# Expanding the last 64 channels for two phases in one step, and issuing every rearrangement copy from SyncE

## The chip, the cores and the metric

The kernel runs on one core of one Trainium2 chip. The metric is the device time of one launch in microseconds (us). The kernel before the change takes 4784.22 us, the median of three runs (4777.77 to 4787.7). A core has five engines with an instruction stream of their own: TensorE (PE in the profile; PEld are its weight loads), VectorE (DVE), ScalarE (ACT), GpSimd (POOL) and SyncE (SP), which issues transfers and computes nothing. Each engine works through its instructions in order and waits where an instruction needs something that isn't there yet.

## The reference

Two residual blocks are applied to 32 images of 96 channels, 56 x 56, in fp32. The first is an inverted bottleneck with weights and activations quantised to 4 bits; the second mixes channels in three ways (a gated 3x3 convolution, a fractional Fourier transform, a Fourier transform) and ends in a dense 3x3 convolution.

```python
# block 1, on _gn(x) (normalised in groups of three channels)
h = bn(conv(x, quant_w(w1), b1, 1, 0, 1), g1, be1, m1, v1)      # 1x1, 96 -> 576
h = act_q(h)                                                    # clip to 0..1, 15 levels
h = bn(conv(h, quant_w(w2), b2, 1, 1, HID), g2, be2, m2, v2)    # 3x3 depthwise, 576
h = act_q(h)
h = bn(conv(h, quant_w(w3), b3, 1, 0, 1), g3, be3, m3, v3)      # 1x1, 576 -> 96
x = x + (_gn(x) + h)
# block 2, on _gn(x), channels in three thirds
#   x_0: 3x3 convolution with gated weights
#   x_05: fractional Fourier transform, 1x1 mix, inverse transform, magnitude
#   x_1: rfft2, 1x1 mix, irfft2
out = conv3x3(concat([x_0, IFRFT, x_1])) + conv2_b
x = x + out
```

## The kernel before

An image is cut into four phases (even and odd rows and columns), 28 x 28 = 784 points each. The 576 hidden channels are cut into five blocks: four of 128 and a last one of 64 (`blk(b)` gives the size). `expand(b, k)` makes block b of phase k. The input is split into a high and a low part, `vh` and `vl`, and both are multiplied by `w1`, so there are 2 x 2 matmuls with 392 columns each. ScalarE evicts the result with scale, offset and Relu (tile `qt`, shown as `qte`), VectorE clips it at 15 and writes it as fp8 into one of three buffers `q1s`. Transfers then rearrange it: the depthwise convolution wants 32 channels of all four phases on 128 partitions, so each group of 32 channels goes into the partitions of its phase in `qp`. Groups are issued from SyncE and GpSimd in turn. For the last block the weight matrix is filled up with zeros to 128 columns, so its steps make 64 channels and 64 rows of nothing.

```python
# weights, once
w1 = cp.tile([C, NB * 128], F32R, tag="w1r", name="w1r")
nc.vector.memset(w1f[:, HID:], 0.0)
nc.vector.tensor_copy(w1, w1f)

def expand(b, k):
    ps = pair(f"pe{i}_{b}_{k}")                       # 2 banks of PSUM; 2 such pairs in all
    for n, v in enumerate((s["vh"], s["vl"])):
        for h in range(2):
            nc.tensor.matmul(ps[:, h, :HN], w1[:, 128 * b : 128 * (b + 1)],
                v[:, k, HN * h : HN * (h + 1)], start=(n == 0), stop=(n == 1))
    src = q1s[turn["q1s"] % 3]
    turn["q1s"] += 1
    quant_act(ps, A1[:, b : b + 1], B1[:, b : b + 1], src[:, :, :PH], f"e{i}_{b}_{k}")
    n, at = blk(b) // G, PW * (k // 2) + k % 2
    for g in range(n):
        (nc.gpsimd if g % 2 else nc.sync).dma_start(
            out=qps[(NB * i + b) % 3][G * k : G * (k + 1), g, at : at + PH * PW],
            in_=src[g * G : (g + 1) * G].rearrange("c h w -> c (h w)"))
```

`depthwise(b, j)` (tile `pd`) reads `qp`, `project` (tile `pp`) comes last in the block. The second block of one image is interleaved with the first block of the next. Its pieces that matter here are these:

```python
def group_stats(stats, name):        # means and 1/std of a group of channels
    ...
    nc.vector.tensor_scalar(ve, pv[:C, 0:1], 1e-5, None, ALU.add)
    nc.gpsimd.tensor_tensor(rstd, ve, mhalf, ALU.pow)      # GpSimd
    ...
def angles():                        # ends with four small transfers
    ...
    nc.sync.dma_start(out=s["xf"][at : at + 1]..., in_=vv[...])
def mix_f(j):                        # matmul pm<-xf,g; two buffers zs; DRAM tile z
    ...
        nc.sync.dma_start(out=s["z"][:, h, at], in_=t)     # z<-zs, 8 per image
    ...
        nc.sync.dma_start(out=zh[...], in_=z[...]...)      # zh<-z, 2 per image
        nc.sync.dma_start(out=az[...], in_=src[r])         # az<-z, 8 per image
# rows_f: matmul pi<-cs,zh, copies to Y;  columns_f: matmul pz<-cs,Y, squares sq, sums Z
# magnitude: four ACT square roots cat<-Z;  final(j): 9 matmuls pc<-cat,wc, x 7 per image
```

The order of the steps:

```python
ex = [(0.75, lambda b=b, k=k: expand(b, k)) for b in range(NB) for k in range(4)]   # 20
de = [(1.45, lambda g=g: depthwise(g // 4, g % 4)) for g in range(NG0)]             # 18
for g in range(NG0):
    conv += de[g : g + 1] + ex[LEAD + g : LEAD + g + 1]                             # LEAD = 7
...
at = 2 * (4 * NB - LEAD) + 1
conv[at:at] = nxt["split"]           # vh and vl of the next image, behind the last expand
```

The framework that builds the program may still move instructions when it lays them out, with a timing model of its own.

Of the kernel before, what the change touches and what calls it, by code (L numbers as in the profile page):

```python
# [37 lines left out]
F32 = mybir.dt.float32  # L38
F32R = mybir.dt.float32r
# [8 lines left out]
C, H, W = 96, 56, 56  # L48
HW = H * W
HID = 576  # L50
NB = 5
# [3 lines left out]
G = 32  # L55
NG0 = HID // G
PH = H // 2
PN = PH * PH
PW = PH + 2
PT = (PH + 1) * PW + 2  # L60
HN = PN // 2
HH = HW // 2
LOW = 64
LEAD = 7
# [13 lines left out]
def blk(b):  # L78
    return 128 if b < NB - 1 else HID - 128 * (NB - 1)


def view(ap, offset, dims):

    return bass.AP(ap.tensor, ap.offset + offset, [list(ap.ap[0])] + [list(d) for d in dims])
# [19 lines left out]
def block_kernel(ctx: ExitStack, tc: tile.TileContext, out: bass.AP, a: dict):  # L104
    nc = tc.nc
# [3 lines left out]
    cp = ctx.enter_context(tc.tile_pool(name="const", bufs=1))  # L109
# [11 lines left out]
    def pair(name):  # L121

        return ps0.tile([128, 2, 512], F32, tag="pair", name=name)
# [4 lines left out]
    def load(i):  # L128
        xt = xp.tile([C, HW], F32, tag="x", name=f"x{i}")
        nc.sync.dma_start(out=xt, in_=x_in[i].rearrange("c h w -> c (h w)"))  # L130
        xts[i] = xt
# [4 lines left out]
    def const(name, eng=nc.scalar):  # L136
        src = a[name]
        t = cp.tile(list(src.shape), F32, tag=name, name=name)
        eng.dma_start(out=t, in_=src)
        return t  # L140

    gmat = const("gmat")
    def prepare():

        room = p1.tile([128, NG0 * PN // 2], F32, tag="q2", name="prep")
        used = [0]

        def tmp(p, n):
            used[0] += n
            return room[:p, used[0] - n : used[0]]  # L150

        def load_tmp(name):
            src = a[name]
            t = tmp(*src.shape)
            nc.scalar.dma_start(out=t, in_=src)
            return t

        def quantise(w, p, n, name):

            w = w[:, :n]  # L160
            nc.scalar.activation(w, w, AF.Tanh)
            mx = tmp(p, 1)
            nc.vector.tensor_reduce(mx, w, AX.X, ALU.max, apply_absolute_value=True)
            am = tmp(p, 1)
            nc.gpsimd.partition_all_reduce(am, mx, p, bass_isa.ReduceOp.max)
            rc = tmp(p, 1)
            nc.vector.tensor_scalar(am, am, 2.0, None, ALU.mult)
            nc.vector.reciprocal(rc, am)
            nc.vector.tensor_scalar(w, w, rc, 0.5, ALU.mult, ALU.add)
            nc.vector.tensor_scalar(w, w, 15.0, MAGIC, ALU.mult, ALU.add)  # L170
            nc.vector.tensor_scalar(w, w, MAGIC, 2.0, ALU.subtract, ALU.mult)
            nc.vector.tensor_scalar(w, w, 15.0, None, ALU.subtract)

        w1f = load_tmp("w1")
        quantise(w1f, C, HID, "1")
        w1 = cp.tile([C, NB * 128], F32R, tag="w1r", name="w1r")
        nc.vector.memset(w1f[:, HID:], 0.0)
        nc.vector.tensor_copy(w1, w1f)
        w2 = load_tmp("w2")
        quantise(w2, 128, NG0 * 16, "2")  # L180
        mask = load_tmp("mask")
        w2v = view(w2, 0, [[16, NG0], [1, 16]])
        nc.vector.tensor_tensor(w2v, w2v, view(mask, 0, [[0, NG0], [1, 16]]), ALU.mult)
        w3f = load_tmp("w3")
        quantise(w3f, 128, NG0 * C, "3")
        w3 = cp.tile([128, NG0, C], BF16, tag="w3q", name="w3q")
        nc.vector.tensor_copy(w3, w3f.rearrange("p (g c) -> p g c", c=C))


        ident4 = load_tmp("ident4")  # L190
        dw = cp.tile([128, NG0, 4, 128], FP8, tag="dw", name="dw")
        for g in range(NG0):
            nc.vector.tensor_tensor(
                view(dw[:, g].rearrange("p t o -> p (t o)"), 0, [[G, 16], [1, G]]),
                view(ident4, 0, [[0, 16], [1, G]]),
                view(w2, 16 * g, [[1, 16], [0, G]]),
                ALU.mult,
                saturate=False,
            )


        v1 = load_tmp("vec1")
        v2 = load_tmp("vec2")
        v3 = load_tmp("vec96")

        def batchnorm(v, p, n, name):
            col = lambda k: v[:, k * n : (k + 1) * n]
            s = cp.tile([p, n], F32, tag=f"s{name}", name=f"s{name}")
            o = cp.tile([p, n], F32, tag=f"o{name}", name=f"o{name}")
            nc.vector.tensor_scalar(s, col(4), BN_EPS, None, ALU.add)  # L210
            nc.scalar.activation(s, s, AF.Sqrt)
            nc.vector.reciprocal(s, s)
            nc.vector.tensor_tensor(s, s, col(1), ALU.mult)
            nc.vector.tensor_tensor(o, col(0), col(3), ALU.subtract)
            nc.vector.tensor_tensor(o, o, s, ALU.mult)
            nc.vector.tensor_tensor(o, o, col(2), ALU.add)
            return s, o

        A1, B1 = batchnorm(v1, 128, NB, "1")
        nc.vector.tensor_scalar(B1, B1, 15.0, None, ALU.mult)  # L220
        A2, B2 = batchnorm(v2, 128, NG0, "2")
        nc.vector.tensor_scalar(A2, A2, 1.0 / 15.0, None, ALU.mult)
        nc.vector.tensor_scalar(B2, B2, 15.0, None, ALU.mult)
        A3, B3 = batchnorm(v3, C, 1, "3")
        nc.vector.tensor_scalar(A3, A3, 1.0 / 225.0, None, ALU.mult)


        def signed(name, factor):
            w = const(name)
            f = load_tmp(factor)  # L230
            nc.vector.tensor_tensor(w, w, f, ALU.mult)
            return w

        cw = signed("cw", "coef")
        return w1, dw, w3, A1, B1, A2, B2, A3, B3, cw

    w1, dw, w3, A1, B1, A2, B2, A3, B3, cw = prepare()
# [14 lines left out]
    q1s, qps = [], []  # L252
# [57 lines left out]
    def quant_act(ps, scale, offset, dst, name):  # L310

        t = p3.tile([128, PN], I16, tag="qt", name=f"qt{name}")
        nc.scalar.activation(t.rearrange("p (h n) -> p h n", h=2), ps[:, :, :HN], AF.Relu, bias=offset, scale=scale)  # L313
        src = t if len(dst.shape) == 2 else t.rearrange("p (h w) -> p h w", w=PH)
        nc.vector.tensor_scalar(dst, src, 15.0, None, ALU.min, saturate=False if dst.dtype == FP8 else None)  # L315
# [9 lines left out]
    def layer0(i):  # L325

        xt = xts[i]
        s = {}
# [37 lines left out]
            nc.vector.tensor_scalar(xt, xt, s["one"], s["off"], ALU.mult, ALU.add)  # L366

        def expand(b, k):
            ps = pair(f"pe{i}_{b}_{k}")
            for n, v in enumerate((s["vh"], s["vl"])):  # L370
                for h in range(2):
                    nc.tensor.matmul(  # L372
                        ps[:, h, :HN],
                        w1[:, 128 * b : 128 * (b + 1)],
                        v[:, k, HN * h : HN * (h + 1)],
                        start=(n == 0),
                        stop=(n == 1),
                    )
            src = q1s[turn["q1s"] % 3]
            turn["q1s"] += 1  # L380
            quant_act(ps, A1[:, b : b + 1], B1[:, b : b + 1], src[:, :, :PH], f"e{i}_{b}_{k}")

            n, at = blk(b) // G, PW * (k // 2) + k % 2
            for g in range(n):
                (nc.gpsimd if g % 2 else nc.sync).dma_start(  # L385
                    out=qps[(NB * i + b) % 3][G * k : G * (k + 1), g, at : at + PH * PW],
                    in_=src[g * G : (g + 1) * G].rearrange("c h w -> c (h w)"),
                )

        def depthwise(b, j):  # L390
            g = 4 * b + j
# [38 lines left out]
                nc.vector.bn_stats(stats2[i][:, j, :], xt[:, j * CN : (j + 1) * CN])  # L430


        ex = [(0.75, lambda b=b, k=k: expand(b, k)) for b in range(NB) for k in range(4)]
        de = [(1.45, lambda g=g: depthwise(g // 4, g % 4)) for g in range(NG0)]
        conv = []
        for g in range(NG0):
# [339 lines left out]
    for i in range(B):  # L776
        conv, nxt = now["conv"], None
        if i + 1 < B:
            nxt = layer0(i + 1)
            conv[8:8] = nxt["norm"]  # L780
            at = 2 * (4 * NB - LEAD) + 1
            conv[at:at] = nxt["split"]


        interleave(conv, one[:-4])
        interleave(now["last"], one[-4:-2])
        head, two, done = layer1(i)
        interleave(head + (nxt["first"] if nxt else []), one[-2:] + end)
        if i + 2 < B:
            load(i + 2)  # L790
        one, end, now = two, done, nxt
# [86 lines left out]
def _layout(inputs):  # L878
# [3 lines left out]
    f = np.float32  # L882
    k = _constants()
# [2 lines left out]

    def hidden(v):

        p = np.zeros((NB * 128,) + v.shape[1:], f)
        p[:HID] = v  # L890
        return np.moveaxis(p.reshape((NB, 128) + v.shape[1:]), 0, 1)

    k["x"] = np.asarray(inputs["x"])
# [34 lines left out]
    start = {"alpha": G, "gfreq": G, "gsp": 0, "gfft": 2 * G}  # L928
# [5 lines left out]
    at = [("gfreq", 0, 64, GO_F), ("gsp", 0, 32, GO_S), ("gfft", 0, 64, GO_T)]  # L934
    at += [("gfreq", 64, 128, GI_F), ("gsp", 32, 64, GI_S), ("gfft", 64, 128, GI_T)]
    for name, lo, hi, to in at:
        n = mlps.index(name)
# [35 lines left out]
```

## Time and profile before

| | value |
|---|---|
| time, median of 3 | 4784.22 us (4777.77 to 4787.7) |
| span of the profiled run, mean granted TensorE clock | 4769.9 us, 0.942 |
| ACT evictions qte of the expand steps | 640, 999 ns mean |
| DVE conversions q1s of the expand steps | 640, 559 ns mean |
| copies qp<-q1s, from SyncE and from GpSimd | 1152 and 1152, 26.2 KB each |
| TensorE matmuls of the expand steps | 2560 (1280 with vh, 1280 with vl) |

The page of the profile gives busy time for each engine and then the groups of instructions: source line, engine, operation, and the tiles in the form written<-read. The waits give, for an instruction, the instruction whose end released it, with the total, the number and the longest. "issue" means that nothing in the profile held the engine back. The granted clock is the share of full speed at which TensorE's clock ran. SPq and POOLq are the queues in which SyncE and GpSimd issue transfers.

### The profile page before, as it was taken

How to read it: one execution, taken by the hardware profiler on the slowest of the kernel's cores; microseconds unless marked ns; L12 is line 12 of the kernel's file. 1: busy time of each engine (PE TensorE's matmuls, PEld its weight loads, DVE VectorE, ACT ScalarE, POOL GpSimd, SP SyncE). 2: the span in 40 equal slices, each digit the busy share in tenths (PEclk: the TensorE clock that was granted, in tenths of full speed). 3: DMA queues.
4: the chain of work that ended last, by engine and by line, in shares of the span. 5: the costliest groups of instructions: out<-in, count | busy, mean ns of one | idle time of the engine just before them, and what ended most of it. 6: DMA issues, size and time to landing. Idle time of an engine off the chain costs nothing.

```text
span 4769.9 us, 60944 instructions
## 1 busy us (share of the span) xinstructions
PE 4327.5 (91%) x21632; PEld 2494.2 (52%) x21632; DVE 2387.7 (50%) x5385; ACT 2166.3 (45%) x2824; POOL 861.2 (18%) x1361
## 2 busy tenths in 40 slices
PE   3899999899999999998999999999999999989987
PEld 2555555555555555555555555455555455555544
DVE  5545544545455555545445454555455444554532
ACT  3544445544445444445444454444454444553431
POOL 3221111221102211112211022111122111122110
PEclk9999999999999999989999989999999999999998
DMA  2221122221122211222211223112222112222112
GB/s 72 44 64 45 38 52 61 65 63 39 35 57 65 64 51 35 48 61 64 63 32 41 58 64 64 43 42 49 61 64 64 45 28 58 63 64 56 30 34 48
DMA packets 378818, 249.65 MB, mean 52 GB/s; under 512 B 283233, under 2 KB 371668, under 8 KB 372372
## 3 DMA queue, kind: packets, MB, share of 16 engines
q1 hardware_dynamic: 339072, 211.72, 20.1%
q0 software_dynamic: 36864, 31.04, 2.8%
q8 instruction: 174, 2.85, 0.3%
q10 hardware_dynamic: 2580, 2.99, 0.2%
q14 instruction: 128, 1.05, 0.1%
HBM read 92.90 MB, written 89.92 MB: 38 GB/s over the span
## 4 chain that ended last, share of the span: by engine, by line
PE 59%; DMA 11%; ACT 10%; DVE 10%; issue 7%; SPq 1%; POOL 1%; DVEq 0%; ACTq 0%; POOLq 0%
PE pc L746 29%; PE pd L398 12%; PE pp L414 5%; PE pe L372 4%; DMA zh<-z 4%; DMA z<-zs 3%; PE pi L678 3%; ACT cat L720 2%; DMA xf<-vv 2%; PE pm L653 2%; ACT qte L313 2%; ACT qtd L313 2%; DVE q1s L315 1%; PE px L616 1%; ACT xm L471 1%
## 5 line engine op out<-in xcount | busy, mean ns | idle before, releaser
L746 PE MATMUL pc<-cat,wc 96*96 96x448 f32 x4032 | 1644.1, 564 | 55.9 <-ACT cat L720 55.9
L385 POOL DMA_DIRECT2D qp<-q1s x1152 | 620.7, 543 | 3621.2 <-issue 1631.1
L746 PEld LDWEIGHTS pc<-cat,wc 96*96 96x96 f32 x4032 | 672.2, 170 | 906.5 <-issue 824.5
L313 ACT ACTIVATE qtd<-pd,o,s 128x784 int16<-128x784 f32 x576 | 576.4, 1001 | 949.8 <-PE pd L398 903.4
L398 PE MATMUL pd<-qp,dw 128*128 128x392 fp8e4 x4608 | 948.6, 350 | 43.3 <-ACT qtd L313 42.0
L313 ACT ACTIVATE qte<-pe,o,s 128x784 int16<-128x784 f32 x640 | 639.2, 999 | 625.5 <-PE pe L372 608.9
L398 PEld LDWEIGHTS <-dw 128*128 128x128 fp8e4 x4608 | 448.0, 101 | 510.5 <-issue 267.9
L372 PE MATMUL pe<-vh,w1r 96*128 96x392 f32 x1280 | 432.1, 420 | 117.4 <-ACT qte L313 63.5
L315 DVE TENSOR_SCALAR q1s<-qte 128x784 fp8e4<-128x784 int16 x640 | 357.4, 559 | 170.8 <-ACT qte L313 120.6
L754 DVE SCALAR_TENSOR_TENSOR x<-pc,bc,x 96x448 f32<-96x448 f32 x224 | 152.3, 680 | 574.5 <-PE pc L746 571.8
L315 DVE TENSOR_SCALAR q<-qtd 128x784 bf16<-128x784 int16 x576 | 207.4, 360 | 406.0 <-ACT qtd L313 405.9
L372 PE MATMUL pe<-vl,w1r 96*128 96x392 f32 x1280 | 352.7, 358 | 0.0
L372 PEld LDWEIGHTS pe<-vh,w1r 96*128 96x128 f32 x1280 | 226.1, 199 | 239.2 <-issue 101.6
L414 PE MATMUL pp<-q,w3q 32*96 32x392 bf16 x4608 | 256.1, 328 | 2.2 <-DVE x L426 2.2
L653 PE MATMUL pm<-xf,g 34*128 34x392 f32 x512 | 202.1, 617 | 56.6 <-DMA xf<-vv 52.8
L372 PEld LDWEIGHTS pe<-vl,w1r 96*128 96x128 f32 x1280 | 246.7, 199 | 0.5
L426 DVE SCALAR_TENSOR_TENSOR x<-pp,s,x 96x392 f32<-96x392 f32 x256 | 142.3, 616 | 176.0 <-PE pp L414 176.0
L414 PEld LDWEIGHTS <-w3q 32*96 32x96 bf16 x4608 | 181.1, 118 | 86.5 <-issue 32.5
L726 PE MATMUL ps<-xq,g 128*128 128x392 f32 x512 | 202.0, 537 | 0.0
L678 PE MATMUL pi<-cs,zh 120*120 120x112 f32 x1024 | 142.3, 302 | 50.3 <-DMA zh<-z 47.2
L361 ACT CAST vh<-v 96x392 fp32r<-96x392 f32 x256 | 126.2, 516 | 130.5 <-DVE v L353 129.7
L333 DVE BATCH_NORM_STATS2 bn<-x 96x6 f32<-96x448 f32 x224 | 121.1, 608 | 123.0 <-DMA x<-in_x_dram 123.0
(150 smaller groups left out, 4072.5 us busy)
## 6 DMA issues: line engine op xcount, KB each, us to landing
z<-zs SPq DMA_DIRECT2D x256, 196.0 KB
x<-in_x_dram SPq DMA_DIRECT2D x32, 1176.0 KB
out_dram<-x SPq DMA_DIRECT2D x32, 1176.0 KB
qp<-q1s SPq DMA_DIRECT2D x1152, 26.2 KB
qp<-q1s POOLq DMA_DIRECT2D x1152, 26.2 KB, 1.9
zh<-z SPq DMA_DIRECT2D x64, 392.0 KB
az<-z SPq DMA_DIRECT2D x256, 98.0 KB
xf<-vv SPq DMA_DIRECT2D x128, 6.1 KB
```

Source lines behind the costliest of these rows:

```text
L313: nc.scalar.activation(t.rearrange("p (h n) -> p h n", h=2), ps[:, :, :HN], AF.Relu, bias=offset, scale=scale)
L315: nc.vector.tensor_scalar(dst, src, 15.0, None, ALU.min, saturate=False if dst.dtype == FP8 else None)
L372: nc.tensor.matmul(ps[:, h, :HN], w1[:, 128 * b : 128 * (b + 1)], v[:, k, HN * h : HN * (h + 1)], start=(n == 0), stop=(n == 1),)
L385: (nc.gpsimd if g % 2 else nc.sync).dma_start(out=qps[(NB * i + b) % 3][G * k : G * (k + 1), g, at : at + PH * PW], in_=src[g * G : (g + 1 ...
L398: nc.tensor.matmul(ps[:, h, :HN], dw[:, g, t, :], view(qps[(NB * i + b) % 3][:, j, :], at, [[PW, PH // 2], [1, PH]]), start=(t == 0), stop ...
L414: nc.tensor.matmul(s["pp"][k // 2][:C, k % 2, :HN], w3[rows, g, :], s["q2"][rows, g, HN * h : HN * (h + 1)], start=(g == 0), stop=(g == NG ...
L426: nc.vector.scalar_tensor_tensor(part, src, A3, part, ALU.mult, ALU.add)
L653: nc.tensor.matmul(ps[:, :HN], g1[rows], s["xf"][rows, at], start=True, stop=True)
L678: nc.tensor.matmul(ps[: LOW + W, 2 * W * k : 2 * W * (k + 1)], zh[:, c : c + 2, :].rearrange("p c w -> p (c w)")[:, : LOW + W], cs, start= ...
L726: nc.tensor.matmul(ps[:, :HN], s["g0"][:, 128 * k : 128 * (k + 1)], view(xq, PH // 2 * h * (W + 2) + k, [[W + 2, PH // 2], [2, PH]]), star ...
L746: nc.tensor.matmul(ps[:C, :CN], wc[:, C * t : C * (t + 1)], cat[:, CR * j + dy : CR * j + dy + CR, dx : dx + W], start=(t == 0), stop=(t = ...
L754: nc.vector.scalar_tensor_tensor(part, ps[:C, :CN], bc, part, ALU.add, ALU.add)
```

## The change

The last block has 64 channels, so two phases of it fit into 128 rows. The new step accumulates both phases in one PSUM pair: for phase k it uses weights with the 64 channels in the left half and zeros in the right, for phase k+1 zeros on the left and the channels on the right. One buffer `w1`, with 64 zero columns on each side of the 64 channels, gives both by a shift of 64 columns. A step of the last block then has 8 matmuls, one eviction and one conversion for two phases, and four copies. The expand steps go from 20 to 18 per image. The scales and offsets of the last block are given twice. All copies are issued from SyncE, GpSimd issues none any more, and the memory kept for GpSimd's transfer descriptors is cut down. The list of steps is two shorter, so the next image's split moves up with it. The aim is fewer evictions and conversions.

```diff
-        w1 = cp.tile([C, NB * 128], F32R, tag="w1r", name="w1r")
-        nc.vector.memset(w1f[:, HID:], 0.0)
-        nc.vector.tensor_copy(w1, w1f)
+        w1 = cp.tile([C, NB * 128 + 64], F32R, tag="w1r", name="w1r")
+        nc.vector.memset(w1[:, HID - 64 :].bitcast(F32), 0.0)
+        nc.vector.tensor_copy(w1[:, : HID - 64], w1f[:, : HID - 64])
+        nc.vector.tensor_copy(w1[:, HID : HID + 64], w1f[:, HID - 64 : HID])
...
         def expand(b, k):
             ps = pair(f"pe{i}_{b}_{k}")
-            for n, v in enumerate((s["vh"], s["vl"])):
+            m = blk(b)
+            n = 128 // m
+            for e in range(2 * n):
                 for h in range(2):
+                    at = 128 * b + m * (n - 1) * (1 - e // 2)
                     nc.tensor.matmul(
                         ps[:, h, :HN],
-                        w1[:, 128 * b : 128 * (b + 1)],
-                        v[:, k, HN * h : HN * (h + 1)],
-                        start=(n == 0),
-                        stop=(n == 1),
+                        w1[:, at : at + 128],
+                        s["vl" if e % 2 else "vh"][:, k + e // 2, HN * h : HN * (h + 1)],
+                        start=(e == 0),
+                        stop=(e == 2 * n - 1),
                     )
...
-            n, at = blk(b) // G, PW * (k // 2) + k % 2
-            for g in range(n):
-                (nc.gpsimd if g % 2 else nc.sync).dma_start(
-                    out=qps[(NB * i + b) % 3][G * k : G * (k + 1), g, at : at + PH * PW],
-                    in_=src[g * G : (g + 1) * G].rearrange("c h w -> c (h w)"),
-                )
+            for u in range(128 // m):
+                at = PW * ((k + u) // 2) + (k + u) % 2
+                for g in range(m // G):
+                    nc.sync.dma_start(
+                        out=qps[(NB * i + b) % 3][G * (k + u) : G * (k + u + 1), g, at : at + PH * PW],
+                        in_=src[m * u + g * G : m * u + (g + 1) * G].rearrange("c h w -> c (h w)"),
+                    )
...
-        ex = [(0.75, lambda b=b, k=k: expand(b, k)) for b in range(NB) for k in range(4)]
+        ex = [(0.75, lambda b=b, k=k: expand(b, k)) for b in range(NB) for k in range(0, 4, 128 // blk(b))]
...
-            at = 2 * (4 * NB - LEAD) + 1
+            at = 2 * (4 * NB - 2 - LEAD) + 1
...
-        p = np.zeros((NB * 128,) + v.shape[1:], f)
-        p[:HID] = v
+        p = np.concatenate([v, v[128 * (NB - 1) :]]).astype(f)
...
-    nc = bacc.Bacc("TRN2", target_bir_lowering=False, num_devices=1)
+    nc = bacc.Bacc("TRN2", target_bir_lowering=False, num_devices=1, dynamic_dma_scratch_size=1024)
```

## The prediction

> **What bounds the kernel now.** I read the page's busy table first, then who TensorE waited for, then one steady image in time, then SyncE's queue.
>
> ```profile
> span 4769.9 us, 60944 instructions
> PE 4327.5 (91%) x21632; PEld 2494.2 (52%) x21632; DVE 2387.7 (50%) x5385; ACT 2166.3 (45%) x2824; POOL 861.2 (18%) x1361
> ```
>
> TensorE is busy for 91% of the span, nothing else for over 52%. The program is bound by matmuls, and a change that leaves them alone can only work on the 440 us in which TensorE idles, and on its clock. The view of waits, for TensorE alone, says what ends that idle time:
>
> ```profile
> PE pe L372 <- ACT qte L313: 63.5, 24, 9.2
> PE pc L746 <- ACT cat L720: 55.9, 32, 3.3
> PE pm L653 <- DMA xf<-vv: 52.8, 30, 3.6
> PE pi L678 <- DMA zh<-z: 47.2, 22, 5.6
> PE pd L398 <- ACT qtd L313: 42.0, 80, 5.1
> PE pe L372 <- DVE x L426: 41.3, 31, 1.3
> ```
>
> (us in total, times, longest.) Put on the time axis, the gaps come back at the same places in each period of about 146 us (31 periods of 137 to 153 us). In the image from 1586.8 us on they are 2.4 us (pe, behind ACT), 1.35 (pm), 1.5 (pi), 1.64 (pc) and 1.3 (pe after pp). [...] The stretches view of the same image:
>
> ```profile
> 1592.00:1595.00 3.00, 3.00 (x10) 1.60 (x10) 1.82 (x5) 0.18 (x2) 1.98 (x5) 0.50 0.28 68
> 1668.10:1720.00 51.90, 50.63 (x274) 24.54 (x274) 21.10 (x40) 11.84 (x17) 0.68 (x1) 0.97 0.01 2
> ```
>
> The third number from the end is the granted clock: right after the 2.4 us gap it is 0.50 and the fp8 matmuls take 0.53 us for 0.34; in the dense stretch it is 0.97. Over the kernel the mean is 0.942, so some 11.6% of the span, 553 us, runs at half clock. That costs at most half of itself, 276 us. [...]
>
> Now the queue that the change loads. SyncE between the vv transfer and the zh load:
>
> ```profile
> 1612.44 3.19 SPq L385 DMA_DIRECT2D qp<-q1s  x3
> 1616.40 0.34 SPq L130 DMA_DIRECT2D x<-in_x_dram  x1
> 1616.79 2.35 SPq L385 DMA_DIRECT2D qp<-q1s  x3
> 1620.43 3.26 SPq L603 DMA_DIRECT2D xf<-vv  x4
> 1629.12 0.57 SPq L385 DMA_DIRECT2D qp<-q1s  x1
> 1629.79 0.52 SPq L658 DMA_DIRECT2D z<-zs  x1
> 1630.37 0.54 SPq L385 DMA_DIRECT2D qp<-q1s  x1
> ...
> 1636.53 2.90 SPq L658 DMA_DIRECT2D z<-zs  x3
> 1639.59 1.28 SPq L385 DMA_DIRECT2D qp<-q1s  x2
> 1642.15 1.39 SPq L663 DMA_DIRECT2D zh<-z  x2
> ```
>
> The copies sit between exactly those transfers (xf, z, zh) for which TensorE waits above.
>
> [...] SyncE spends 0.54 us (median of 1152) on a copy whose last packet is through 1.5 us after the issue began. [...] the trace has 1.9 us from issue to landing for GpSimd's copies[...]. [...] The slow stretches in this trace last 3.4, 6.8, 10.2 or 13.7 us. [...] The trace shows nothing to gain: q1s takes 0.549 us beside a GpSimd copy and 0.563 without.
>
> **The change, part by part.**
>
> *TensorE.* Block 4 has 16 matmuls per image now (4 phases x 2 parts x 2 halves) and 16 after (2 steps x 4 x 2), same 96x128 weights, same 392 columns. Change in TensorE work: 0.
>
> *Evictions.* Two of 20 steps go per image: 64 ACT evictions of 1.0 us and 64 VectorE conversions of 0.56 us, 64 us and 36 us of engines that are half idle. What counts is where they lie. Counting the pe groups of one image, the last four steps start 75.4, 82.7, 84.8 and 93.1 us after 1572.3, and the first pc matmul of the next 3x3 convolution at 95.8. So they lie in the chain that ends in the pc gap: the chain of waits there runs ACT qte 1.01, DVE q1s 0.57, DMA qp 1.65, DVE q1s 0.56, then sq, Z, the table load 1.28 and four cat of 0.87. Taking two steps out should shorten it by one to two us; but TensorE has only the 1.64 us gap to win. Over the kernel the pe-to-pc gaps are 49.6 us. I count two thirds, 33 us. In about 15 images a 3.4 us slow stretch starts at this gap, worth 1.7 us each if it goes: 15 of 25 us. **-48 us.**
>
> *GpSimd freed.* It issues 1152 copies of 0.54 us in order, and the rstd power waits behind them: VectorE has veb ready at 1579.12, GpSimd starts the power at 1581.20 after six copies, and ACT's four xm/xq (6.75 us) start at 1582.13, ahead of the qte for which TensorE waits 2.4 us. Without the copies the power could come 2 us earlier. Against it, VectorE is in order, and q1s number four (waiting 1.39 us for a copy until 1580.52) precedes the use of the power; that copy lands about 0.2 us later when four issue in a row from 1577.35 (last start 1579.15, plus 1.5). If the order of instructions stays, 0.4 us is won; if the power's user moves ahead, 2 us. The pe-to-pe gaps are 68.7 us; half is 34. The slow stretches behind them are the longest (153 us in all, at most 76 us of cost): a third of that, 25. **-59 us.**
>
> *SyncE loaded.* Copies go from 36 to 72 per image, 0.6 us each with the pause between two: 22 to 43 us of 146, so SyncE isn't full on average. Locally it is. From 1612.44 to the xf transfers it issues six copies and has 2.8 us free; six more need 3.6 us, so xf starts at least 0.8 us late, more where a copy is held up for 2 us behind the 1.2 MB store, as one was at 1613.00. I take 1.1 us x 30 images that wait there: 33 us. From 1629.12 to 1639.43 it issues eight z stores and six copies, 7.2 us of 10.3 with pauses; six more make 10.8. The window can't hold them, and a z store that comes late delays the next zs, since two buffers alternate (ACT and DVE waited 263 us for z stores). I take 1.8 us until the zh load. About 28 images have no slack for it: 50 us. Longer gaps in pm and pi lengthen slow stretches: 0.8 us an image, 25 us. The x load (8 us until landing) and the extra copies behind it in one queue: 15 us. **+123 us.**
>
> *Next image's split* moves ahead by two depthwise groups, into a stretch without a gap: 0.
>
> Sum: -48 - 59 + 123 = +16 us, **4784 + 16 = 4800 us**.
>
> **The rivals.** (1) Nothing matters, TensorE is the bound: 4784. For it: 91% busy, unchanged matmuls. Against it: every removed or added wait above sits in a gap. (2) Relief wins: the order of instructions adapts, copies stay out of the z stores' way, and the pe and pc gaps go with their slow stretches. That is 49.6 + 68.7 + 25 + about 50, at best 190 us, less some loss on SyncE: 4620 to 4700. For it: the transfers are now finely interleaved with the copies, so the order was chosen with the issue times in view. (3) SyncE becomes the bound of the xf, z and zh chain: 2.6 us at zh and 1.3 at xf in all images, with slow stretches after both, and nothing won: 4784 + 125 + 80, about 4990 at worst, 4900 more likely. For it: the overfull window. Against it: TensorE has depthwise and expand work that can fill a later zh.
>
> **Range and chances.** Gain and loss are each near 110 us and each uncertain by about half, 55 us; together some 75 us, and 1.28 times that is 95. I take 4710 to 4890. 2% is 96 us: below 4689 is 1.5 of these spreads from 4800, above 4880 1.07. With some weight for rival 2: 0.15 faster, 0.64 same, 0.21 slower.
>
> **What would show it.** TensorE's busy time at 4327 us up to clock changes, with 21632 matmuls. ACT qte 576 evictions for 640. The wait pc <- ACT cat down from 55.9 to about 20; pe <- ACT qte down from 63.5 to 30 or so; pm <- xf up from 52.8 to 85; pi <- zh up from 47.2 to about 100. SyncE issuing all 2304 copies. The mean clock near 0.94. I am wrong if zh or xf waits don't grow (SyncE had room), if the pe wait grows (the copies' landing throttles the three q1s buffers), or if the clock moves by over 0.01.

## The result and the profile after

The changed kernel takes 4920.75 us (median of 4 runs, 4902.85 to 4929.86) against 4784.02 us before: a ratio of 1.0283 with a 95% interval of 1.0251 to 1.0314. The prediction had 4800 us and a range of 4710 to 4890; the measured time lies above it.

The page of the changed kernel, its span and the table of busy time by engine:

```profile
span 4915.4 us, 59718 instructions
PE 4339.1 (88%) x21632; PEld 2498.4 (51%) x21632; DVE 2355.1 (48%) x5322; ACT 2123.1 (43%) x2760; POOL 176.8 (4%) x209
```

TensorE's busy time is 11.6 us higher with the same 21632 matmuls, GpSimd is down to 209 instructions, ACT has 64 fewer. So 134 of the 145.5 us by which the span grew are time in which TensorE stands still. The view of waits for TensorE after the change (total us, times, longest):

```profile
PE pc L753 <- ACT cat L727: 199.8, 32, 6.8
PE pm L660 <- DVE bn L335: 101.9, 27, 5.1
...
PE pi L685 <- DMA zh<-z: 31.4, 17, 4.1
...
PE pe L378 <- ACT qte L315: 18.4, 5, 9.1
```

Against the rows of before, pc went from 55.9 to 199.8, pm from 52.8 to 101.9 under another releaser, pi fell from 47.2 to 31.4 and pe from 63.5 to 18.4. Summing TensorE's gaps in the trace by the tile before and after them (for each place the commonest pair) gives the same account: into pc 49.6 to 196.8 us (+147), into pm 50.5 to 110.2 (+60), between pe groups 68.7 to 16.5 (-52), into pi 41.6 to 34.3 (-7), the rest -14; together +134.

The largest item is the start of the 3x3 convolution. VectorE in the changed kernel, in order of time, in one image ahead of it (start, duration, line, operation, out<-in, count):

```profile
1716.55 0.62 DVE L719 TENSOR_TENSOR sq<-pz,az 128x448 f32<-128x448 f32 x1
1717.09 0.56 DVE L317 TENSOR_SCALAR q1s<-qte 128x784 fp8e4<-128x784 int16 x1
1717.56 0.56 DVE L364 TENSOR_TENSOR vl<-v,vh 96x392 fp32r<-96x392 f32 x1
1718.04 0.61 DVE L719 TENSOR_TENSOR sq<-pz,az 128x448 f32<-128x448 f32 x1
1718.57 0.55 DVE L364 TENSOR_TENSOR vl<-v,vh 96x392 fp32r<-96x392 f32 x1
1719.05 0.47 DVE L355 TENSOR_SCALAR v<-x,sta 96x392 f32<-96x392 f32 x1
1719.44 0.38 DVE L722 TENSOR_TENSOR Z<-sq 128x224 f32<-128x224 f32 x1
1719.74 0.87 DVE L355 TENSOR_SCALAR v<-x,sta 96x392 f32<-96x392 f32 x2
...
1725.35 0.26 DVE L722 TENSOR_TENSOR Z<-sq 128x112 f32<-128x112 f32 x1
```

The rows v and vl, and vh below, are the next image's split, and they stand between sq and Z, which the convolution needs. ACT shows the same, with vh between its squares, and then the four square roots:

```profile
1720.25 0.94 ACT L363 CAST vh<-v 96x392 fp32r<-96x392 f32 x2 [0.18 <-DVE v L355]
1721.54 0.58 ACT L720 ACTIVATE sq<-sq 128x448 f32<-128x448 f32 x1 [0.35 <-DVE sq L719]
...
1726.12 1.28 ACT L727 ACT_TABLE_LOAD   x1
1727.41 3.50 ACT L727 ACTIVATE cat<-Z 32x784 f32<-32x784 f32 x4
```

From the first sq on VectorE to the end of the last cat it takes 14.36 us here, median of 32 images; before it took 8.75. The stretches view of the two kernels for this part, before first (columns: busy us and instructions of PE, PEld, DVE, ACT, POOL, then the granted clock):

```profile
1659.30:1668.10 8.80, 7.16 (x40) 4.92 (x40) 4.21 (x10) 6.93 (x11) 0.50 (x1) 1.00 0.03 7
```

```profile
1716.50:1730.90 14.40, 7.78 (x44) 4.94 (x42) 12.98 (x27) 11.80 (x20) 0.00 (x0) 0.95 0.08 19
1731.00:1738.00 7.00, 7.00 (x12) 2.88 (x13) 0.73 (x2) 1.84 (x2) 0.00 (x0) 0.62 0.00 0
```

TensorE has 7 to 8 us of work in both. VectorE goes from 4.21 us of work in 8.80 to 12.98 in 14.40 and is nearly full. The next row shows what stands behind the gap: the clock is at 0.62 over the first 7 us of the convolution, where it was at 0.76 before the change (1668.10 to 1675.10).

The second item is the vv transfer. SyncE in the changed kernel, around the x load:

```profile
1668.32 0.33 SPq L130 DMA_DIRECT2D x<-in_x_dram  x1
1668.75 4.83 SPq L392 DMA_DIRECT2D qp<-q1s  x7
1677.01 3.27 SPq L610 DMA_DIRECT2D xf<-vv  x4
```

vv was ready at 1672.03, SyncE was through with its seven copies at 1673.58, and xf starts at 1677.01, just after the x load landed at 1676.94. SyncE's own waits name that load:

```profile
SPq L610 <- DMA x<-in_x_dram: 91.1, 29, 4.1
```

xf reads nothing of x. But SyncE's transfers take eight completion semaphores in turn, as the semaphore numbers in the trace show (eight different ones; in 3061 of 3064 cases a transfer has that of the eighth ahead of it), and the instruction just ahead of the first xf is a wait for the semaphore of the load. The load took the first, seven copies the others, so xf needs the load's own; 29 of the 32 loads have an xf as the eighth transfer behind them. Before the change there were three copies in that place, and xf waited for nothing but vv.

### The profile page after: what moved, and what is told of

The parts are those of the page before. It is cut to its first block, busy times and chain, and to the rows that moved or that the text cites. A ratio compares the mean times of both kernels' runs of the same rounds, so it can differ in the third digit from the quotient of the medians.

```text
span 4915.4 us, 59718 instructions
## 1 busy us (share of the span) xinstructions
PE 4339.1 (88%) x21632; PEld 2498.4 (51%) x21632; DVE 2355.1 (48%) x5322; ACT 2123.1 (43%) x2760; POOL 176.8 (4%) x209
## 4 chain that ended last, share of the span: by engine, by line
PE 62%; DVE 16%; DMA 9%; ACT 6%; issue 4%; SPq 2%; POOL 0%; DVEq 0%; ACTq 0%; POOLq 0%
PE pc L753 31%; PE pd L405 12%; PE pp L421 5%; PE pe L378 4%; PE pm L660 4%; DMA qp<-q1s 3%; DMA zh<-z 3%; PE pi L685 3%; SPq L392 2%; DVE bn L335 2%; DMA x<-in_x_dram 2%; DVE vl L364 2%; ACT cat L727 2%; DMA z<-zs 2%; DVE x L433 1%
## 5 line engine op out<-in xcount | busy, mean ns | idle before, releaser
L753 PE MATMUL pc<-cat,wc 96*96 96x448 f32 x4032 | 1669.3, 570 | 199.8 <-ACT cat L727 199.8
L315 ACT ACTIVATE qte<-pe,o,s 128x784 int16<-128x784 f32 x576 | 573.1, 1000 | 694.5 <-PE pe L378 678.0
L317 DVE TENSOR_SCALAR q1s<-qte 128x784 fp8e4<-128x784 int16 x576 | 322.4, 561 | 219.6 <-ACT qte L315 110.4
L660 PE MATMUL pm<-xf,g 34*128 34x392 f32 x512 | 205.9, 782 | 112.7 <-DVE bn L335 101.9
L335 DVE BATCH_NORM_STATS2 bn<-x 96x6 f32<-96x448 f32 x224 | 121.1, 607 | 136.7 <-DMA x<-in_x_dram 136.7
L685 PE MATMUL pi<-cs,zh 120*120 120x112 f32 x1024 | 140.1, 299 | 38.4 <-DMA zh<-z 31.4
L660 PEld LDWEIGHTS pm<-xf,g 34*128 34x128 f32 x512 | 71.2, 266 | 184.2 <-DVE bn L335 110.0
L685 PEld LDWEIGHTS pi<-cs,zh 120*120 120x120 f32 x1024 | 134.9, 213 | 49.3 <-DVE q1s L317 21.4
```

The lines of the kernel that those rows point to most:

```text
L335: nc.vector.bn_stats(stats[:, j, :], xt[:, j * CN : (j + 1) * CN])
L660: nc.tensor.matmul(ps[:, :HN], g1[rows], s["xf"][rows, at], start=True, stop=True)
L685: nc.tensor.matmul(ps[: LOW + W, 2 * W * k : 2 * W * (k + 1)], zh[:, c : c + 2, :].rearrange("p c w -> p (c w)")[:, : LOW + W], cs, start= ...
L753: nc.tensor.matmul(ps[:C, :CN], wc[:, C * t : C * (t + 1)], cat[:, CR * j + dy : CR * j + dy + CR, dx : dx + W], start=(t == 0), stop=(t = ...
```

## The experiments

Theory S: the split, moved ahead with the shorter list, stands in the sq, Z, cat chain and holds up the 3x3 convolution. Theory Q, the rival: SyncE's longer queue is the cause. Both would also show as waits elsewhere, so each half of the change was undone alone, and both together. All times are compared with runs of the kernel before on the same chip.

**The split where it stood before (e1).**

```diff
-            at = 2 * (4 * NB - 2 - LEAD) + 1
+            at = 2 * (4 * NB - 2 - LEAD) + 1 + 2
```

> The changed kernel, with the next image's split put two depthwise groups later, where it stood before the change. Theory S (the split's VectorE and ScalarE work now stands inside the sq, Z, cat chain and holds up the 3x3 convolution): pc <- cat falls from 200 us to about 60, time from 4921 to 4770 +- 30. Theory Q (SyncE's longer queue is the cause, through xf, z and zh): pc <- cat stays near 200, time 4900 to 4920.

4707.02 us against 4781.92: ratio 0.9853 (0.9834 to 0.9872). TensorE's waits, in part:

```profile
PE pi L685 <- DMA zh<-z: 49.8, 25, 4.8
PE pc L753 <- ACT cat L727: 39.9, 32, 6.5
```

The wait of pc falls from 199.8 to 39.9 us. Changing one index in a list turns a loss of 2.8% into a gain of 1.5%. It is 63 us faster than the middle of what I expected: TensorE's busy time falls as well, from 4339 to 4293 us, with the half-clock stretches down from 758 to 634. SyncE's queue is untouched, so theory Q falls as the main cause.

**The copies in turn again, the split early (e2).** Both engines issue, so the memory for GpSimd's descriptors is set to 8192, here and in all later versions of the changed kernel in which GpSimd issues transfers.

```diff
-                    nc.sync.dma_start(
+                    (nc.gpsimd if g % 2 else nc.sync).dma_start(
...
-    dynamic_dma_scratch_size=1024
+    dynamic_dma_scratch_size=8192
```

> The changed kernel with the copies issued by SyncE and GpSimd in turn again, split where the change put it. Theory S: pc <- cat stays near 200; pm <- bn goes from 102 back to pm <- xf near 50; pe <- qte comes back from 18 to about 60; time 4890 +- 30. Theory Q: nearly all is regained, 4780 +- 30.

4951.55 us, ratio 1.0345 (1.0301 to 1.0389), slower than the changed kernel itself. The waits of its TensorE:

```profile
PE pc L753 <- ACT cat L727: 199.6, 32, 6.8
PE pe L378 <- ACT qte L315: 88.2, 31, 9.2
PE pm L660 <- DMA xf<-vv: 48.0, 30, 3.0
```

pc is as bad as in the changed kernel, pm is back at 48, and pe is back and worse. My 4890 was too low: I had pc and pm right, but pe at about 60 us where it is 88.2. Theory Q expected 4780.

**Both undone, 18 steps kept (e3).** The two edits above together.

> Both undone, only the 18 steps left of the change. Theory S with the xf wait as a second cause: 4740 +- 30, under the kernel before, since the pc gap shrinks by one to two us an image. If the two-phase step itself costs time (8 matmuls hold a PSUM pair longer): 4784 or more.

4685.59 us, ratio 0.9800 (0.9771 to 0.9829). The two-phase step itself is worth 96 us. Of TensorE's gaps, counted as above, pe to pe goes from 68.7 to 32.6 us, into pc from 49.6 to 29.4, into pi from 41.6 to 28.0, into pmb from 28.0 to 15.8; busy time is the same within 3 us.

**SyncE alone, 20 steps (e4).** The kernel before with this edit only:

```diff
-                (nc.gpsimd if g % 2 else nc.sync).dma_start(
+                nc.sync.dma_start(
```

> The kernel before with 20 steps, all copies issued by SyncE and nothing else changed. Theory S: SyncE alone costs the xf wait (+60) and wins the pe wait (-50): 4795 +- 30. Theory Q: 4900 +- 30.

4758.81 us, ratio 0.9956 (0.9944 to 0.9968). Its waits:

```profile
PE pm L653 <- DVE bn L333: 105.4, 29, 4.7
PE pi L678 <- DMA zh<-z: 60.5, 28, 4.5
PE pc L746 <- ACT cat L720: 60.5, 32, 6.7
```

The pm wait doubles, as in the changed kernel, pi gains 13 us, and the pe wait for qte falls from 63.5 us to 18.3. SyncE alone is a small gain, where I had +64 us (-59 for GpSimd, +123 for SyncE). With 18 steps and the late split it is a small loss instead: e1 is 21 us over e3.

**What holds xf (e5, e6).** Theory L: the completion semaphore of the x load. Theory B: VectorE works in order (in the trace of the changed kernel its 5322 instructions start in the program's order, as do SyncE's 3072 and GpSimd's 209), stands at bn (the statistics of the next image's x) until x has landed, and so can't copy PQ, the result of the matmuls ahead of pm, out of PSUM. In e5 the x load is issued by GpSimd; e6 has the statistics four entries later. Both have the late split.

```diff
# e5
-        nc.sync.dma_start(out=xt, in_=x_in[i]...)
+        (nc.gpsimd if i > 1 else nc.sync).dma_start(out=xt, in_=x_in[i]...)
# e6
-            conv[8:8] = nxt["norm"]
+            conv[12:12] = nxt["norm"]
```

> Late split, all copies on SyncE, but the x load (from the third image on) issued by GpSimd, so that SyncE's xf transfers no longer share a completion semaphore and a queue with it. Theory L (xf is held in SyncE until the x load has landed, because SyncE's transfers take eight completion semaphores in turn and xf is the eighth after the load): the SyncE wait xf <- x goes from 91 us to 0, the pe-to-pm gap from 106 to about 50, time from 4707 to 4640 +- 25. Theory B (VectorE, in order, stands at bn waiting for x and can't copy PQ): the gap stays near 100, time 4700 +- 25.

4743.09 us, ratio 0.9911 (0.9886 to 0.9936): slower than e1, with TensorE busy 4376 us for 4293 and 758 us at half clock for 634. SyncE's waits in e5, in part:

```profile
SPq L610 <- DMA qp<-q1s: 60.3, 46, 2.8
```

and TensorE's:

```profile
PE pm L660 <- DMA xf<-vv: 84.9, 27, 4.0
```

The wait for x is gone, and a wait for the copies has taken its place. The mean time from vv ready to the first xf issue (first and last two images left out) falls only from 4.28 to 2.41 us, the four issues take 4.87 for 3.28, and the gap into pm stays at 96 us. So the load's semaphore was the holder that the trace named, but not the only one: the copies beside the load are late too (in the changed kernel those issued behind it before it has landed land 6.48 us after their issue began, the others 1.85, medians of 203 and 2021), and theirs come next.

> Late split, all copies on SyncE, but the next image's statistics (bn, which wait for x) put four entries later in the list. Theory B: VectorE's wait for x (137 us) and the pe-to-pm gap (106) shrink to under 60, time 4640 to 4670. Theory L: VectorE's wait shrinks, the pm gap stays at 90 to 110 behind xf, time 4700 +- 25.

4905.78 us, ratio 1.0259 (1.0237 to 1.0281). TensorE's largest wait shows where:

```profile
PE pc L753 <- ACT cat L727: 178.9, 32, 6.0
```

and VectorE's, in part:

```profile
DVE bn L335 <- DMA x<-in_x_dram: 135.2, 31, 7.6
```

VectorE's wait for x is as long as ever: the edit did not move bn there, so e6 says nothing for or against theory B. It is an unplanned test of theory S instead. The list has the split late, but in the program that came out 20 of its operations stand between the first sq and the last cat, and the chain takes 13.62 us. Medians over the images of all runs so far:

| run | split operations in the chain | chain, us | gap into pc, us |
|---|---|---|---|
| before | 1 | 8.75 | 49.6 |
| e4 | 1 | 8.76 | 50.7 |
| changed kernel | 22 | 14.36 | 196.8 |
| e2 | 22 | 14.36 | 196.1 |
| e6 | 20 | 13.62 | 174.8 |
| e1 | 1 | 8.76 | 36.4 |
| e3 | 1 | 8.75 | 29.4 |

In the changed kernel and e2 it is 21 in some images and 22 in the others. What counts is the order in which the operations stand on the engines, not the entry in the list.

**The split later still (e7).**

```diff
-            at = 2 * (4 * NB - 2 - LEAD) + 1
+            at = 2 * (4 * NB - 2 - LEAD) + 1 + 4
```

> All copies on SyncE, the split four entries later than in the changed kernel (two later than before the change). Theory S: pc <- cat stays at 35 to 50 as with two later, since the split is already out of the cat chain; time 4707 +- 20. If only the number of steps between mattered and not the chain: it goes on falling by some 50 us.

4691.72 us, ratio 0.9806 (0.9788 to 0.9824), with no split operation in the chain (8.75 us) and 30.7 us into pc. Once it is out, more distance buys little, as theory S has it.

**Statistics later, copies in turn (e8).** The edit of e6 on e3.

> Late split, copies from SyncE and GpSimd in turn, statistics four entries later. A try at a better version: 4686 before the step; under theory B up to 40 less, under theory L no change within 15.

4774.08 us, ratio 0.9989 (0.9968 to 1.0010). Here the chain stays clean (8.75 us), but TensorE's wait of pi for zh goes to 96.3 us. A miss as a better version; why zh comes later with the statistics moved was not tried.

**xf on an engine with semaphores of its own (e9).** Before the change GpSimd's 1152 copies take eight other semaphores than SyncE's 1920 transfers, as the trace shows, and GpSimd's xf transfers in the program of e9 have those eight again. e7 with

```diff
-                    nc.sync.dma_start(
+                    nc.gpsimd.dma_start(
                         out=s["xf"][at : at + 1]...
```

> As e7 (split four entries later, all copies on SyncE), with the four small xf transfers issued by GpSimd, which has completion semaphores of its own. Theory L in its wider form (xf is held because a completion semaphore is used again only when its last transfer, load or copy, has landed, and everything lands late beside the x load): the time from vv ready to the first xf issue goes from 4.4 us to under 0.5, the pe-to-pm gap from 109 to 30 to 60, time from 4692 to 4630 +- 25. If xf is late for another reason (the transfer itself is slow beside the x load): gap 90 to 110, 4690 +- 20.

4675.42 us, ratio 0.9764 (0.9729 to 0.9799). GpSimd in order of time, at one image's xf:

```profile
1599.08 2.12 POOL L610 DMA_DIRECT2D xf<-vv  x4 [30.54 <-DVE vv L606]
```

and TensorE's wait for it:

```profile
PE pm L660 <- DMA xf<-vv: 57.0, 30, 3.0
```

From vv ready to the first issue it is 0.29 us for 4.37, and the gap into pm falls from 109.0 to 55.8 us: theory L in its wider form holds. Theory B falls: VectorE waits for x as long as ever (135.9 us, 136.7 in the changed kernel), yet pm starts while bn still runs in all 29 images where the two meet. The waits of the changed kernel name bn because it ends at almost the same time as xf: in the image shown above the later of the two xf transfers that the first pm needs landed at 1680.68, bn ended at 1680.76, and pm started at 1680.82. In 30 of the 31 images with such a gap, pm starts 0.14 us (median) after that landing, and so it does in e9.

The time gains less than the gap: 16 us between the medians. The ratios, 0.9806 and 0.9764, have overlapping intervals, so a gain in time is not certain. In the traces TensorE's busy time rises by 38 us (4278 to 4316). That this is the clock is not shown: in this run the half-clock stretches add up to 546 us, fewer than the 601 of e7.

**The best place of the split with the copies in turn (e10), and with xf on GpSimd as well (e11).**

> As e7, with the copies from SyncE and GpSimd in turn: like e3 (4686), pm gap near 50, time 4670 +- 20.

4675.66 us, ratio 0.9771 (0.9741 to 0.9802), level with e9.

> e10 with xf from GpSimd, which now issues half of the copies as well: xf was not held in e3, so theory L expects no gain, 4670 +- 20.

4738.57 us, ratio 0.9892 (0.9848 to 0.9936). xf wasn't held in e10 (0.03 us from vv to issue, 0.39 in e11), so no gain was expected, but the loss of 63 us was not. TensorE's gaps are the same (348 and 345 us); its busy time is 4364 us for 4301, with 709 us at half clock for 535. What tipped the clock stays open.

The best versions, e9 and e10, are 2.3% under the kernel before and 5% under the changed one.

## Why the prediction was wrong

*"Next image's split moves ahead by two depthwise groups, into a stretch without a gap: 0."* This is the step that failed. The stretch had no gap for the split's sake, but VectorE and ACT carry the chain from pz to cat there, and the split is 24 operations and a pass over x on just these two engines. In the changed kernel 21 or 22 of them landed in the chain and lengthened it by 5.6 us, in 29 of the 32 images; TensorE had only 7.78 us of work for the 14.40. Undoing this alone (e1) takes the ratio from 1.0283 to 0.9853, and the gap into pc from 196.8 to 36.4 us. So the split cost some 214 us, and the rest of my sum, +16, measured -75 us: with the split where it stood before, the time is 4707 us, just under my range. The profile of before held the warning: of the 1.64 us gaps into pc I read that the chain sets the start of the convolution, and I counted what the change takes out of it, but not what it puts in. I looked at the split for its input (after the last expand) and not for its engines, of which ACT was already busy for 6.93 us of the 8.80.

*TensorE's work: 0.* Right: 21632 matmuls, and busy time up 0.3%.

*Evictions: -48 us.* The evictions fell by 64 as counted. With the split late and the copies in turn (e3) the two-phase step is worth -96 us. The gap into pc gave 20 us where I had 33; the pe to pe gap, 36 us smaller, had no part in my sum. No run tried why it shrinks with two steps fewer, but the traces have a hint: it follows the time that the rstd power on GpSimd waits once veb is ready. The medians are 2.21 us in e2 (gap 92.8), 2.02 before (68.7), 1.58 in e10 (45.1), 0.95 in e3 (32.6) and 0.14 with all copies on SyncE (16 to 19).

*GpSimd freed: -59 us.* The pe to pe gap fell by 52 us, half more than the 34 I allowed, and e4 has the same. The power's user did move ahead: ACT's xm starts 1.07 us after veb for 3.01 before (medians), and the conversion q1s that stood in between no longer does.

*SyncE loaded: +123 us.* Wrong in size and in mechanism. I had xf late by 1.1 us for the issue time of six more copies; it was late by 4.3 us, held by a completion semaphore, and the gap into pm grew by 60 us, not 33. I had zh late by 1.8 us and 50 us of gap; the pi wait grew by 13 us in e4 and fell in the changed kernel, so the "overfull window" was mostly absorbed. The 1.5 us that I took to a SyncE copy's landing are those to its last packet: by its semaphore a SyncE copy lands 2.01 us after its issue began, a GpSimd copy 1.92 (medians of 1152 each, before), so SyncE's copies land no sooner. GpSimd and SyncE together came to -23 us in e4, not +64.

*The clock.* I expected a mean near 0.94; it is 0.923. I had called a move of over 0.01 a sign of being wrong. The stretches at half clock grew from 553 to 758 us, and they sit behind the two gaps that grew: 324 us of them start behind the gap from pe into pm (106 before), 235 us behind the gap into pc (44 before). Those behind pe to pe, 154 us before, are gone. Why TensorE's busy time grew by only 12 us under 205 us more of half clock is not shown. Nor is it shown how long TensorE has to idle ahead of such a stretch: before the change, 77 of the 87 stretches have no gap as long as the shortest of them (3.4 us) in the 6 us ahead of them, and in half of them TensorE idled for under 1.7 us of the last 3.4. And not every gap has one behind it: in the image of the prediction the clock is 1.00 over the 3 us behind the gap into pi (1.5 us) and over 4 us behind the one after pp (1.3 us). One stretch lasts 20.5 us, longer than those I listed.

*The rivals.* None was the split. Rival 3 named the right size (4900) for the wrong reason; e4 and e2 refute it as the cause. Rival 2 (4620 to 4700) is about what the change gives when the split stays out of the way: 4707 in e1, 4692 in e7. The relief at pe and pc came, but the slow stretches did not go: 634 us at half clock in e1, 553 before.

## What to carry to other kernels

When a list of steps gets shorter, whatever is anchored to its end moves as well: look up on which engines the moved piece works, and who needs those engines where it lands, not only whether its inputs are ready. Count how many of its operations stand inside the chain that sets the end there: here 20 to 22 made it 4.9 to 5.6 us longer, and the entry in the program's list did not fix that number. When many small transfers go to one engine, ask also which transfer an urgent one shares its completion semaphore with (here xf with the load eight ahead of it: 4.3 us).

## What the runs showed of the hardware that was not expected

A transfer can be held in its issuing engine by one it has nothing to do with. With all copies on SyncE the four small xf transfers were issued 4.3 us after their data was ready, because the 1.2 MB load eight transfers earlier hadn't landed (a load lands 8.24 us after its issue, median of 32); on GpSimd, which has semaphores of its own, it took 0.29 us. So issuing from a second engine saves more than issue time in this program, because it also separates the semaphores: 4 us of delay (4.37 us in e7, 0.29 in e9) against 0.8 us of issue for each of those transfers (3.27 us for four). The wait is an instruction of the program, which reuses eight semaphores in turn; no run here has another way of handing them out.

Two kernels with the same gaps on TensorE can differ by 1.3%: e10 and e11 have 345 and 348 us of gaps and 63 us between their medians, all of it in TensorE's busy time under a mean clock of 0.943 and 0.925.
